# Layer 1 of a four-layer convolution kernel: weight preparation moved into the first convolution and the main loop, statistics regrouped within SBUF, one channel summed without a DMA

## The chip, the cores and the metric

The kernel runs on one core of a Trainium2 chip. The metric is the device time of the whole program in microseconds (us), from which each change is judged. One execution of the kernel before was also taken by the hardware profiler; every time below that names an engine or an instruction comes from that execution, counted from the start of its span.

## The reference, cut to what matters

Four layers follow each other on x of shape (4, 128, 64, 64), float32: an attention layer (layer 0), layer 1, a transformer-like block (layer 2) and a state-space layer (layer 3). The change touches layer 1 alone. Layer 1 is, twice, a 3x3 convolution with weights rounded to powers of two and then an "adder" convolution, each time with a batch norm behind it:

```python
def shift_quant(w, threshold=0.005):
    aw = jnp.abs(w)
    q = jnp.sign(w) * jnp.exp2(jnp.round(jnp.log2(jnp.maximum(aw, 1e-10))))
    q = jnp.where(aw < threshold, 0.0, q)
    return w + lax.stop_gradient(q - w)
...
def per_channel(wc):                       # adder_conv: p = 3x3 patches of all 128 channels
    return -jnp.sum(jnp.abs(p - wc[None, :, None]), axis=1)
...
out = adder_conv(shift_conv(x, w_shift1), w_add1)
out = jax.nn.relu(batchnorm(out, bn1_gamma, bn1_beta))     # statistics over all images and pixels
out = adder_conv(shift_conv(out, w_shift2), w_add2)
out = batchnorm(out, bn2_gamma, bn2_beta)
return jax.nn.relu(out + residual)
```

An output channel of the adder convolution sums 9 taps x 128 input channels of absolute differences for each pixel.

## The kernel before, in words

Each half of layer 1 is one call of `shift_adder`, the first with the prefix `a1`, the second with `a2`; the prefixes stand in the tile names of the profile. The three places that the change touches are where layer 0 hands over to `a1`, where `a1` hands over to `a2`, and where `a2` hands over to layer 2. They are called the first, second and third edge here.

**Before `a1`.** `layer1` calls `quantized` twice: load one set of shift weights (128 x 1152, tile `a1ws`, then `a2ws`), run nine VectorE instructions on it (`quantize`, L266 to L278), leave the result in `a1wq`, `a2wq`. Both calls use a small pool of their own over the same addresses.

**Start of `shift_adder`.** It loads the adder weights `wa` (L306), makes six negated copies `wn` (L311), fills small constant tiles (`pick`, `third`, L316 to L320), and forms `wsum`, sums of the weights over input channels, by 16 accumulations of six one-column matmuls each (L335) that VectorE copies from PSUM (L339). A float32 matmul shows as two in the profile, so these are 192 there. `w_third` (L328, L329) is one weight plane with only every fourth output channel kept. It lies in a pool of its own, closed before the pool of the convolution's input tiles (`xin`) is opened over the same addresses.

**Convolution of image 0.** `convolution(0)` is a generator: for each of 8 blocks of 512 pixels it fetches rows (`xin`, three buffers; in `a2` `normed` scales them on VectorE, L574, and ScalarE, L575), issues nine matmuls, yielding after each, and copies the block from PSUM into the padded image `pb` (L380). Image 0's runs by itself. Those of images 1 to 3 run beside the main loop.

**Main loop.** It goes over 4 images x 128 output channels, four channels at a time, in the order that the list `ORDER` writes out by hand. ScalarE makes absolute differences (`aa`, L456), VectorE makes maxima (`da`, L470; `ma`, L479; and L462), and TensorE sums each stream over the input channels with one-hot `pick` weights into PSUM (`pa`, L425). For the two `PAIR_TAPS` of a channel, `pair` makes two `ma` tiles for each half image, and a DMA issued by GpSimd adds one to the other (L481), so that TensorE need sum only one. An entry `0C0` of `ORDER` advances three steps of `beside`: the 12 steps of `sums_of_p` (a matmul sum over the image itself) and the 72 of the next image's convolution. There are 31 such entries per image that find work allowed, so 93 steps, of which 84 are used on images 0 to 2.

**Evacuation and statistics.** After 32 channels (a chunk) `evacuate` adds `wsum` and `sps` to each PSUM half (L437), takes `bn_stats` (L440) and stores to `y1d` or `y2d` in DRAM (L442). After the last chunk `batchnorm_scale` stores the statistics tile to DRAM (`stats_d`, L543), loads it back regrouped by channel (`byco`, L546), aggregates it (L550) and forms the scale `sc` (L83, L84, L553).

**Order.** A scheduler places instructions by readiness and by order in the program; `tc.keep_in_program_order` (called `then`) pins an instruction behind the one traced before it on its engine. [...] A pool opened over addresses of a closed pool waits for that pool's last users. [...]

Of the kernel before, what the change touches and what calls it, by code (L numbers as in the profile page):

```python
# [9 lines left out]
F32 = mybir.dt.float32  # L10
I32 = mybir.dt.int32
AF = mybir.ActivationFunctionType
ALU = mybir.AluOpType
# [248 lines left out]
def quantize(nc, sb, w, of, name):  # L262

    flat = [P, TAPS * P]
    aw = sb.tile(flat, F32, tag="qa", name=f"{name}_aw")
    nc.vector.tensor_scalar(aw.bitcast(I32), w.bitcast(I32), 0x7FFFFFFF, None, ALU.bitwise_and)  # L266

    pw = sb.tile(flat, F32, tag="qp", name=f"{name}_pw")
    nc.vector.tensor_scalar(pw.bitcast(I32), w.bitcast(I32), 0x7F800000, None, ALU.bitwise_and)
    up = sb.tile(flat, F32, tag="qu", name=f"{name}_up")  # L270
    nc.vector.scalar_tensor_tensor(up, pw, 1.4142135381698608, aw, ALU.mult, ALU.is_lt)
    nc.vector.scalar_tensor_tensor(pw, up, 1.0, pw, ALU.add, ALU.mult)
    nc.vector.scalar_tensor_tensor(pw, aw, 0.005, pw, ALU.is_ge, ALU.mult)
    sg = sb.tile(flat, I32, tag="qu", name=f"{name}_sg")
    nc.vector.tensor_scalar(sg, w.bitcast(I32), -0x80000000, None, ALU.bitwise_and)
    nc.vector.tensor_tensor(pw.bitcast(I32), pw.bitcast(I32), sg, ALU.bitwise_or)
    nc.vector.tensor_tensor(pw, pw, w, ALU.subtract)
    nc.vector.tensor_tensor(of, w, pw, ALU.add)  # L278


def quantized(tc, pool, w_shift, tag):

    nc = tc.nc
    wqs = pool.tile([P, TAPS, P], F32, name=f"{tag}wq")
    with tc.tile_pool(name=f"{tag}q", bufs=1) as qp:
        ws = qp.tile([P, TAPS * P], F32, name=f"{tag}ws")
        nc.sync.dma_start(ws, w_shift)
        quantize(nc, qp, ws, wqs.rearrange("p t o -> p (t o)"), tag)
    return wqs


def shift_adder(tc, cm, load, wqs, w_add, stats, y_d, tag):
# [10 lines left out]
    with ExitStack() as ctx:  # L303
        cp = ctx.enter_context(tc.tile_pool(name=f"{tag}c", bufs=1))
        wa = cp.tile([P, TAPS, P], F32, name=f"{tag}wa")
        nc.sync.dma_start(wa.rearrange("p t o -> p (t o)"), w_add)  # L306
        wn = {}
        for t, scale in [(t, 1.0) for t in ABS_TAPS[0]] + [(ABS_TAPS[c][i], 0.5) for c, i in HALF.items()]:
            if (t, scale) not in wn:
                wn[t, scale] = cp.tile([P, P], F32, name=f"{tag}wn{t}_{len(wn)}")  # L310
                nc.vector.tensor_scalar(wn[t, scale], wa[:, t, :], -scale, None, ALU.mult)  # L311

        pick = {}
        for v in (-1.0, -2.0):
            pick[v] = cp.tile([P, 63], F32, name=f"{tag}pick{int(-v)}")
            nc.vector.memset(pick[v], 0.0)  # L316
            nc.vector.memset(pick[v][:, 31:32], v)
        third = cp.tile([P, 32], F32, name=f"{tag}third")
        nc.vector.memset(third, 0.0)
        nc.vector.memset(third[:, 2:32:4], 1.0)  # L320
# [5 lines left out]
        with tc.tile_pool(name=f"{tag}w", bufs=1) as wt:  # L326
            w_third = wt.tile([P, P], F32, name=f"{tag}wthird")
            nc.vector.memset(w_third, 0.0)  # L328
            nc.vector.tensor_copy(w_third[:, 2:P:4], wa[:, MAX_TAPS[3], 2:P:4])  # L329
            pw = ps_c.tile([P, NC], F32, tag="cv", name=f"{tag}pw")  # L330
            for c in range(NC):
                for g in range(4):
                    for i, t in enumerate(sum_taps):
                        w = w_third if t == MAX_TAPS[3] else wa[:, t, :]
                        nc.tensor.matmul(  # L335
                            pw[32 * g : 32 * g + 32, c : c + 1], w[:, 32 * c : 32 * c + 32], cm.one_col,
                            start=(i == 0), stop=(i == len(sum_taps) - 1), skip_group_check=True,
                        )
            nc.vector.tensor_copy(wsum, pw)  # L339
# [64 lines left out]
        def beside(b, pb_of):  # L404

            yield from sums_of_p(b, pb_of[b], sp_of[b])
            if b < B - 1:
                pb_of[b + 1] = padded(b + 1)
                yield from convolution(b + 1, pb_of[b + 1])

        pb_of, sp_of = {0: padded(0)}, {}
        for _ in convolution(0, pb_of[0]):
            pass
# [19 lines left out]
        def evacuate(chunk):  # L433
            b, c = divmod(chunk, NC)
            for k in range(2):
                o = ep.tile([P, BK], F32, tag="ev", name=f"{tag}ev{b}_{c}_{k}")
                then(nc.vector.scalar_tensor_tensor(  # L437
                    o, pa_of[chunk][k], wsum[:, c : c + 1], sp_of[b][:, k, :], ALU.add, ALU.add
                ))
                then(nc.vector.bn_stats(stats[:, c, 2 * b + k, :], o))  # L440
                to = y_d[b, 32 * c : 32 * c + 32, :].rearrange("j (k g w) -> k g j w", k=2, g=4)
                nc.sync.dma_start(to[k], o)  # L442

# [29 lines left out]
        def pair(n, h):  # L473

            ms = []
            for t in PAIR_TAPS:
                mt = mp.tile([P, HL], F32, tag="am", name=f"m{tag}_{n}_{t}_{h}")
                v = view(n, t, h * H // 2, (h + 1) * H // 2)
                then(nc.vector.tensor_scalar(rows(mt), v, weight(n, t), None, ALU.max))  # L479
                ms.append(mt)  # L480
            then(nc.gpsimd.dma_start(ms[1], ms[0], accum_op=ALU.add))  # L481
            streams[n, "p", h] = (-2.0, ms[1], (h,))
# [52 lines left out]
def layer1(ctx, tc, cm, w_shift1, w_add1, g1, b1, w_shift2, w_add2, g2, b2, x1d, y1d, y2d, stats_d):  # L535
# [5 lines left out]
    def batchnorm_scale(stats, at, gamma, name):  # L541

        nc.sync.dma_start(at, stats.rearrange("p c s v -> p c (s v)"))  # L543
        byco = lp.tile([P, 4, 2 * B * 6], F32, name=f"byco{name}")
        for c in range(4):
            nc.sync.dma_start(  # L546
                byco[32 * c : 32 * c + 32], at[:, c, :].rearrange("(g j) s -> j g s", g=4)
            )
        mv = cm.pool.tile([P, 2], F32, name=f"mv{name}")
        nc.vector.bn_aggr(mv, byco.rearrange("p g s -> p (g s)"))  # L550
        sc = cm.pool.tile([P, 1], F32, name=f"sc{name}")
        cm.rstd(nc, sc, mv[:, 1:2])
        nc.vector.tensor_tensor(sc, sc, gamma, ALU.mult)  # L553
        return mv[:, 0:1], sc
# [5 lines left out]
    wq1, wq2 = quantized(tc, lp, w_shift1, "a1"), quantized(tc, lp, w_shift2, "a2")  # L560
# [6 lines left out]
    shift_adder(tc, cm, plain, wq1, w_add1, stats1, y1d, "a1")  # L567
    mean1, sc1 = batchnorm_scale(stats1, stats_d[0], vec["g1"], "1")
# [11 lines left out]
    shift_adder(tc, cm, normed, wq2, w_add2, stats2, y2d, "a2")  # L580
    mean2, sc2 = batchnorm_scale(stats2, stats_d[1], vec["g2"], "2")
# [997 lines left out]
def kernel(ctx: ExitStack, tc: tile.TileContext, i: dict, out: bass.AP):  # L1579
# [5 lines left out]
    stats_d = dp.tile([2, P, 4, 2 * B * 6], F32, name="stats_d")  # L1585
# [16 lines left out]
        i["w_shift2"], i["w_add2"], i["bn2_gamma"], i["bn2_beta"], x1d, y1d, y2d, stats_d,  # L1602
# [112 lines left out]
```

## Time and profile before

| What | us |
|---|---|
| Median of three runs | 21133.91 |
| The three runs | 21133.91, 21114.99, 21178.35 |
| Profiled execution, own time | 21155.93 |
| Span of that execution | 21154.1 |
| Layer 0's last VectorE instruction ends | 1980.1 |
| `a1`: first convolution matmul, first main-loop instruction | 2025.02, 2090.76 |
| `a2`: first convolution matmul, first main-loop instruction | 9438.45, 9504.25 |
| Last `a2` sum on TensorE starts | 16848.66 |
| First scaling of layer 2's input (L673) | 16878.51 |

The profile page gives TensorE as busy for 93% of the span, VectorE 90%, ScalarE 83%. Lines of the timeline read: start, busy time, engine, source line, operation, output <- inputs, shapes, count; in brackets the idle time of the engine before it and what ended that. Engine names with a q are sequencers, which wait for semaphores and issue DMAs.

### The profile page before, as it was taken

How to read it: one execution, taken by the hardware profiler on the slowest of the kernel's cores; microseconds unless marked ns; L12 is line 12 of the kernel's file. 1: busy time of each engine (PE TensorE's matmuls, PEld its weight loads, DVE VectorE, ACT ScalarE, POOL GpSimd, SP SyncE). 2: the span in 40 equal slices, each digit the busy share in tenths (PEclk: the TensorE clock that was granted, in tenths of full speed). 3: DMA queues.
4: the chain of work that ended last, by engine and by line, in shares of the span. 5: the costliest groups of instructions: out<-in, count | busy, mean ns of one | idle time of the engine just before them, and what ended most of it. 6: DMA issues, size and time to landing. Idle time of an engine off the chain costs nothing.

```text
span 21154.1 us, 323001 instructions
## 1 busy us (share of the span) xinstructions
PE 19660.1 (93%) x139180; PEld 6292.0 (30%) x139180; DVE 18970.2 (90%) x12273; ACT 17550.0 (83%) x9055; POOL 7577.3 (36%) x3844
## 2 busy tenths in 40 slices
PE   9998999999999999999999999999999877789998
PEld 4443222222222222222222222222222223223333
DVE  7876999999999999989999999999999887799998
ACT  5664999999999999989999999999999833466666
POOL 5665222222222222212222222222222100189998
PEclk9999999999999999999999999999999988699999
DMA  0000777777777777767777777777777710389997
GB/s 13 9 9 20 147 152 148 147 154 149 151 145 152 150 143 151 156 136 145 150 148 152 149 148 151 147 149 147 147 154 153 162 21 20 130 238 251 253 253 218
DMA packets 576191, 2970.17 MB, mean 140 GB/s; under 512 B 164572, under 2 KB 165476, under 8 KB 240804
## 3 DMA queue, kind: packets, MB, share of 16 engines
q0 software_dynamic: 296800, 2160.20, 51.0%
q1 hardware_dynamic: 277812, 787.19, 13.0%
q8 instruction: 1089, 17.84, 0.3%
q14 instruction: 346, 2.83, 0.0%
q10 hardware_dynamic: 144, 2.10, 0.0%
HBM read 662.03 MB, written 128.78 MB: 37 GB/s over the span
## 4 chain that ended last, share of the span: by engine, by line
PE 43%; issue 15%; DMA 14%; DVE 14%; ACT 11%; POOL 3%; SPq 1%; DVEq 0%; POOLq 0%; ACTq 0%
PE a1pa L425 15%; PE a2pa L425 13%; DMA ma<-ma 10%; ACT aa L456 9%; PE pe L164 4%; PE pav L207 4%; DVE h L1364 4%; DVE ma L479 3%; DVE da L470 2%; DMA du<-du_d 2%; DVE g L854 1%; POOL ma L481 1%; PE mg L1379 1%; DMA dl<-delta_d 1%; PE a1pc L375 1%
## 5 line engine op out<-in xcount | busy, mean ns | idle before, releaser
L481 POOL DMA_DIRECT2D ma<-ma x2048 | 3799.7, 1870 | 10892.9 <-DVE ma L479 7671.8
L456 ACT ACTIVATE aa<-a1pb,a1wn 128x4096 f32<-128x4096 f32 x1920 | 6959.4, 3711 | 485.5 <-PE a1pa L425 342.0
L456 ACT ACTIVATE aa<-a2pb,a2wn 128x4096 f32<-128x4096 f32 x1920 | 6964.9, 3712 | 358.9 <-PE a2pa L425 340.4
L425 PE MATMUL a1pa<-aa,a1pick 128*32 128x512 f32 x30720 | 3616.8, 600 | 84.4 <-ACT aa L456 81.3
L425 PE MATMUL a2pa<-aa,a2pick 128*32 128x512 f32 x30720 | 3617.2, 600 | 82.6 <-ACT aa L456 81.3
L470 DVE TENSOR_SCALAR da<-a2pb,a2wa 128x4096 f32<-128x4096 f32 x1408 | 3271.0, 2350 | 316.1 <-PE a2pa L425 316.1
L470 DVE TENSOR_SCALAR da<-a1pb,a1wa 128x4096 f32<-128x4096 f32 x1408 | 3269.6, 2350 | 306.8 <-PE a1pa L425 306.5
L425 PE MATMUL a1pa<-da,a1pick 128*32 128x512 f32 x22528 | 2696.1, 597 | 15.2 <-DVE da L470 15.2
L425 PE MATMUL a2pa<-da,a2pick 128*32 128x512 f32 x22528 | 2680.8, 594 | 18.0 <-DVE da L470 18.0
L479 DVE TENSOR_SCALAR ma<-a1pb,a1wa 128x2048 f32<-128x2048 f32 x2048 | 2529.8, 1282 | 71.1 <-DMA ma<-ma 71.1
L479 DVE TENSOR_SCALAR ma<-a2pb,a2wa 128x2048 f32<-128x2048 f32 x2048 | 2530.6, 1282 | 63.5 <-DMA ma<-ma 63.3
L1379 PE MATMUL mg<-h,ident 128*128 128x512 f32 x4096 | 1955.8, 615 | 214.6 <-ACT m L1388 174.0
L1364 DVE TENSOR_TENSOR_SCAN h<-da,h,dbu 128x1024 f32<-128x1024 f32 x768 | 1804.3, 2349 | 126.1 <-ACT da L1350 32.2
L425 PEld LDWEIGHTS a1pa<-aa,a1pick 128*32 128x32 f32 x30720 | 982.4, 111 | 2492.5 <-issue 2130.5
L425 PEld LDWEIGHTS a2pa<-aa,a2pick 128*32 128x32 f32 x30720 | 983.1, 111 | 2488.0 <-issue 2132.9
L425 PE MATMUL a2pa<-ma,a2pick 128*32 128x512 f32 x8192 | 1094.2, 607 | 266.0 <-DMA ma<-ma 265.8
L425 PE MATMUL a1pa<-ma,a1pick 128*32 128x512 f32 x8192 | 1096.2, 608 | 239.1 <-DMA ma<-ma 239.1
L201 POOL TENSOR_TENSOR ssum<-ssum,et 128x512 f32<-128x512 f32 x960 | 1230.0, 1281 | 233.0 <-ACT et L196 166.1
L425 PEld LDWEIGHTS a1pa<-da,a1pick 128*32 128x32 f32 x22528 | 716.9, 110 | 1747.2 <-issue 1612.4
L425 PEld LDWEIGHTS a2pa<-da,a2pick 128*32 128x32 f32 x22528 | 714.8, 110 | 1739.7 <-issue 1584.1
L462 DVE SCALAR_TENSOR_TENSOR aa<-a2pb,a2wa,aa 128x4096 f32<-128x4096 f32 x256 | 1147.4, 4482 | 81.8 <-ACT aa L456 81.7
L462 DVE SCALAR_TENSOR_TENSOR aa<-a1pb,a1wa,aa 128x4096 f32<-128x4096 f32 x256 | 1147.4, 4482 | 78.2 <-ACT aa L456 78.0
(295 smaller groups left out, 17707.1 us busy)
## 6 DMA issues: line engine op xcount, KB each, us to landing
ma<-ma POOLq DMA_DIRECT2D x2048, 1024.0 KB, 8.9
dl<-delta_d SPq DMA_DIRECT2D x256, 512.0 KB
dl<-delta_d SPq DMA_DIRECT2D x512, 256.0 KB
du<-du_d SPq DMA_DIRECT2D x256, 512.0 KB
du<-du_d SPq DMA_DIRECT2D x512, 256.0 KB
sz_d<-sz SPq DMA_DIRECT2D x64, 256.0 KB
xs_d<-xs SPq DMA_DIRECT2D x8, 2048.0 KB
delta_d<-dv SPq DMA_DIRECT2D x32, 512.0 KB
```

Of the source, the lines that this page charges most:

```text
L164: nc.tensor.matmul(pe, k[:, bass.ts(j, P)], unit[u, "q"], start=True, stop=True)
L201: nc.gpsimd.tensor_tensor(unit[u, "sum"], unit[u, "sum"], at, ALU.add)
L207: nc.tensor.matmul(unit[u, "av"], image[u // NB][2][:, j, :], at, start=(j == 0), stop=(j == NJ - 1))
L375: then(nc.tensor.matmul(pc, wqs[:, t, :], here[:, y : y + RB, x : x + W], start=(t == 0), stop=(t == TAPS - 1),))
L425: then(nc.tensor.matmul(pa[k][32 * g : 32 * g + 32, :], pick[v][:, 31 - jj : 63 - jj], d[:, bass.ts(4 * at + g, BK)], start=(n // 32, k) n ...
L456: then(nc.scalar.activation(rows(at), view(n, t), AF.Abs, bias=bias, scale=scale))
L462: then(nc.vector.scalar_tensor_tensor(rows(at), view(n, ADDED_TAP), weight(n, ADDED_TAP), rows(at), ALU.max, ALU.add))
L470: then(nc.vector.tensor_scalar(rows(dt), view(n, t), weight(n, t), None, ALU.max))
L479: then(nc.vector.tensor_scalar(rows(mt), v, weight(n, t), None, ALU.max))
L481: then(nc.gpsimd.dma_start(ms[1], ms[0], accum_op=ALU.add))
L1364: then(nc.vector.tensor_tensor_scan(t[:, cols][:, s], da[:, s], st[n, "dbu", h][:, cols][:, s], 0.0 if e % 4 == 0 else st["last"], ALU.mul ...
L1379: then(nc.tensor.matmul(pm, cm.ident, st[n, way, h][:, bass.ts(k, BK)], start=(way == 0), stop=(way == 1)))
```

## The change

It has four parts.

1. `quantize` becomes a generator that takes four `am` buffers (the main loop's pool for `ma` tiles, seven buffers) instead of a pool of its own, and `shift_adder` runs it. The first set is quantized ahead of `a1`'s first convolution. The second set's load is issued after that convolution's first matmul, and its VectorE instructions come in four portions at later matmuls of it. `a2` quantizes nothing.
2. The load of `wa`, the negated copies and `w_third` are likewise placed inside the convolution of image 0; the matmuls of `wsum` become eight steps of `beside` for image 0, behind `sums_of_p`. `pick` and `third` are filled by GpSimd instead of VectorE. `w_third` lives in a buffer of the evacuation pool.
3. The statistics no longer go through DRAM. When the last image's chunk is evacuated, four DMAs copy its rows of `stats` directly into `byco`; the last chunk's odd two are issued by ScalarE's queue.
4. For the very last channel `pair` issues no summing DMA; both `ma` tiles become streams that TensorE sums.

```diff
-def quantized(tc, pool, w_shift, tag):
...
-def shift_adder(tc, cm, load, wqs, w_add, stats, y_d, tag):
+def quantize(tc, pool, w_shift, of, name):
     nc = tc.nc
+    then = tc.keep_in_program_order
+    w, aw, pw, up = [
+        pool.tile([P, HL], F32, tag="am", name=f"{name}_q{k}")[:, 0 : TAPS * P] for k in range(4)
+    ]
+    nc.sync.dma_start(w, w_shift)
+    yield
...
+def shift_adder(tc, cm, load, wqs, shifts, w_add, stats, byco, y_d, tag):
...
-        nc.sync.dma_start(wa.rearrange("p t o -> p (t o)"), w_add)
         wn = {}
...
-            nc.vector.memset(pick[v], 0.0)
-            nc.vector.memset(pick[v][:, 31:32], v)
+            nc.gpsimd.memset(pick[v], 0.0)
+            nc.gpsimd.memset(pick[v][:, 31:32], v)
...
+        def sums_of_w(w_third):
             pw = ps_c.tile([P, NC], F32, tag="cv", name=f"{tag}pw")
             for c in range(NC):
                 for g in range(4):
...
+                    if g % 2:
+                        yield
+            then(nc.vector.tensor_copy(wsum, pw))
...
             yield from sums_of_p(b, pb_of[b], sp_of[b])
+            if b == 0:
+                yield from sums_of_w(w_third)
...
-        for _ in convolution(0, pb_of[0]):
-            pass
+        quantizing = [quantize(tc, mp, w, of, f"{tag}{k}") for k, (w, of) in enumerate(shifts)]
+        for q in quantizing[:1]:
+            for _ in q:
+                pass
+        for at, _ in enumerate(convolution(0, pb_of[0])):
+            if at == 0:
+                nc.sync.dma_start(wa.rearrange("p t o -> p (t o)"), w_add)
+                for q in quantizing[1:]:
+                    next(q)
+            if at % TAPS == 4 and at > 2 * TAPS:
+                for q in quantizing[1:]:
+                    next(q, None)
+            if at == 2 * TAPS + 1:
+                negated()
+                w_third = ep.tile([P, BK], F32, tag="ev", name=f"{tag}wthird")[:, 0:P]
+                then(nc.gpsimd.memset(w_third, 0.0))
+                then(nc.vector.tensor_copy(w_third[:, 2:P:4], wa[:, MAX_TAPS[3], 2:P:4]))
...
+            if b == B - 1:
+                for g in range(4):
+                    (nc.scalar if c == NC - 1 and g % 2 else nc.sync).dma_start(
+                        byco[32 * c : 32 * c + 32, g, :],
+                        stats[32 * g : 32 * g + 32, c, :, :].rearrange("p s v -> p (s v)"),
+                    )
...
-            then(nc.gpsimd.dma_start(ms[1], ms[0], accum_op=ALU.add))
+            if n < B * P - 1:
+                then(nc.gpsimd.dma_start(ms[1], ms[0], accum_op=ALU.add))
+            else:
+                streams[n, "q", h] = (-2.0, ms[0], (h,))
             streams[n, "p", h] = (-2.0, ms[1], (h,))
...
-        nc.sync.dma_start(at, stats.rearrange("p c s v -> p c (s v)"))
-        byco = lp.tile([P, 4, 2 * B * 6], F32, name=f"byco{name}")
-        for c in range(4):
-            nc.sync.dma_start(
-                byco[32 * c : 32 * c + 32], at[:, c, :].rearrange("(g j) s -> j g s", g=4)
-            )
...
-    shift_adder(tc, cm, plain, wq1, w_add1, stats1, y1d, "a1")
+    shift_adder(tc, cm, plain, wq[0], shifts, w_add1, stats1, byco[0], y1d, "a1")
...
-    shift_adder(tc, cm, normed, wq2, w_add2, stats2, y2d, "a2")
+    shift_adder(tc, cm, normed, wq[1], (), w_add2, stats2, byco[1], y2d, "a2")
```

## Prediction

> **What bounds the kernel now.** I read the page's busy shares first, then its chain, then the timeline of each engine around the three edges, then sums over stretches of the main loop. In the main loop ScalarE and TensorE are both full, so nothing large can come from there. The edges are different: they are chains in which one engine works and the rest wait.
>
> First edge, timeline of VectorE, and below it of TensorE:
>
> ```profile
> 1984.41 0.76 DVE L266 TENSOR_SCALAR a_aw<-a1ws 128x1152 int32<-128x1152 int32 x1 [4.29 <-DMA a1ws<-in_w_shift]
> ...
> 1998.59 0.76 DVE L266 TENSOR_SCALAR a_aw<-a2ws 128x1152 int32<-128x1152 int32 x1 [3.72 <-DMA a2ws<-in_w_shift]
> ...
> 2012.76 0.91 DVE L311 TENSOR_SCALAR a1wn<-a1wa 128x128 f32<-128x128 f32 x6 [3.16 <-DMA a1wa<-in_w_add]
> ...
> 2021.01 0.16 DVE L339 COPY a1wsum<-a1pw 128x4 f32<-128x4 f32 x1 [7.24 <-PE a1pw L335]
> 2035.85 0.69 DVE L380 COPY a1pb<-a1pc 128x512 f32<-128x512 f32 x1 [14.68 <-PE a1pc L375]
> ```
> ```profile
> 2025.02 50.28 PE L375 MATMUL a1pc<-a1xin,a1wq 128*128 128x512 f32 x110 [4.04 <-DMA a1xin<-x1d]
> ```
>
> Load, quantize, load, quantize, load, sum, load, convolve, one after the other. The first quantization ends at 1994.87 (L278 starts at 1993.51, 1.36 long), yet the convolution that needs only it starts at 2025.02.
>
> Second edge: TensorE, SyncE, VectorE.
>
> ```profile
> 9413.31 1.93 PE L425 MATMUL a1pa<-ma,a1pick 128*32 128x512 f32 x8 [5.49 <-DMA ma<-ma]
> ...
> 9438.45 65.03 PE L375 MATMUL a2pc<-a2xin,a2wq 128*128 128x512 f32 x144 [5.67 <-ACT a2xin L575]
> ```
> ```profile
> 9416.84 0.34 SPq L543 DMA_DIRECT2D stats_d<-stats  x1
> ...
> 9423.03 1.75 SPq L546 DMA_DIRECT2D byco<-stats_d  x4
> 9432.85 71.13 SPq L571 DMA_DIRECT2D a2xin<-y1d  x11
> ```
> ```profile
> 9426.16 1.02 DVE L550 BATCH_NORM_AGGREGATE mv<-byco 128x2 f32<-128x192 f32 x1 [0.58 <-DMA byco<-stats_d]
> 9432.82 0.16 DVE L339 COPY a2wsum<-a2pw 128x4 f32<-128x4 f32 x1 [5.64 <-PE a2pw L335]
> ```
>
> The last sum waits for a DMA, the statistics for a round trip through DRAM (6.2 us from 9416.84 to 9423.03), and `xin` for `wsum`.
>
> Third edge: SyncE, then VectorE.
>
> ```profile
> 16852.18 1.10 SPq L543 DMA_DIRECT2D stats_d<-stats  x1
> ...
> 16860.99 0.47 SPq L623 DMA_DIRECT2D dwb<-in_dw_b  x1
> 16863.85 1.76 SPq L546 DMA_DIRECT2D byco<-stats_d  x4
> ...
> 16869.77 1.76 SPq L671 DMA_DIRECT2D x<-y2d  x4
> ```
> ```profile
> 16867.13 1.02 DVE L550 BATCH_NORM_AGGREGATE mv<-byco 128x2 f32<-128x192 f32 x1 [15.00 <-DMA byco<-stats_d]
> ...
> 16878.51 2.41 DVE L673 TENSOR_SCALAR x<-x,mv,sc 128x4096 f32<-128x4096 f32 x1 [6.44 <-DMA x<-y2d]
> ```
>
> The wait list puts SyncE's stop before L623 down to `res` (5.7 us), a 2 MB load that ScalarE issues at 16850.65. Layer 2's weight loads follow, and only then `x`.
>
> [...] SyncE's 256 KB store of 16851.57 moves its packets from 16858.60 on, when `res` is nearly through. [...] The first block takes 10.83 us (2025.02 to 2035.85), later ones 7.73, and I keep that penalty.
>
> **First edge, part by part.** The `am` pool overlaps layer 0's pools, so its first load goes where `a1ws` went, 1980.56. Nine instructions end at 1994.87. The first input rows are then long there: their load, 4.0 us in the old place, runs beside quantization. So is `wa` (3.7 us). GpSimd fills the constants beside it too. Convolution starts at 1995.0 instead of 2025.02: **-30.0**. Removed are a load and a quantization (1994.87 to 2009.07, 14.2), `wa` and its sums (11.9), the wait for `xin` (4.0). Added to VectorE within the convolution are 10.5 us of quantization, 0.91 of negation, 0.19 for `w_third`. It has 7.0 us free between block copies, the largest portion is 2.9 us, and three PSUM buffers stand between it and TensorE: nothing. Without that cover it would be 11.6 us. SyncE gets two loads ahead of later `xin` rows, which are needed 7.73 us apart: nothing. If the first load is slowed by those queued behind it, 2 us; nothing excludes 1 us of gain from an earlier landing. I take 0.
>
> **Second edge.** Before the last two channel sums, TensorE ran `ma` of 510 at 9404.95. Then come four half-image streams of eight matmuls instead of two: 4 x 0.86 = 3.4 us, no DMA awaited, the last `ma` tile being done at 9405.6. They end at 9409.4, where the old end was 9415.24. Evacuation and statistics are done at 9411.0 (before: 9416.77), 5.8 earlier. The `byco` copies leave at 9411.1, two per queue 0.5 us apart, behind a 256 KB store. No SBUF-to-SBUF copy of this size is in the trace; the load of L546 took 1.8 us from its last issue to L550. I take 2.0, keep 1.5 and 6.2 as ends, and get L550 at 9413.5 and, 3.0 us on as before, `sc` at 9416.5. Beside it GpSimd, free of `a1`'s constants at 9410.3, spends about 1.7 us on memsets; `xin` goes out at 9412.0 and lands 3.9 us later (as 9432.85 to 9436.76), at 9415.9. Scaling starts at 9416.6, the convolution 1.7 later: 9418.3 instead of 9438.45, **-20.2**. Ends -16 and -21.
>
> **Third edge.** TensorE ends 5.8 us earlier by the same four streams, at 16844.8, and `res` leaves then. It took 10.3 us (16850.65 to 16860.99), so it is through at 16855.1, with the `byco` copies just behind it and L550 at about 16856.5. SyncE still stops at the DMA eight places after `res`, now the first of twelve weight loads (0.48 us each, 5.8): `x` leaves at 16860.9, against 16869.77. **-8.9**; -12 if the stop falls among later loads, -3 if the copies wait longer.
>
> **Main loop.** The sums of weights are 192 short passes in 7.9 us (41 ns each), now in the first image of each half. TensorE has little room: over 22 groups of four channels,
>
> ```profile
> 2437.10:3691.90 1254.80, 1217.71 (x10696) 360.03 (x10692) 1180.74 (x659) 1196.39 (x331) 324.52 (x183) 0.99 0.75 151
> ...
> 7960.10:9181.60 1221.50, 1156.70 (x10564) 335.18 (x10560) 1175.42 (x652) 1196.10 (x331) 274.96 (x176) 0.99 0.76 154
> 9849.00:11121.20 1272.20, 1218.20 (x10696) 357.43 (x10692) 1185.67 (x666) 1202.38 (x338) 344.76 (x182) 0.99 0.74 149
> ...
> 15400.60:16615.20 1214.60, 1151.75 (x10564) 334.40 (x10560) 1175.23 (x651) 1195.51 (x331) 278.59 (x176) 0.99 0.77 154
> ```
>
> (stretch and its length, then the busy times of PE, PEld, DVE, ACT and POOL). Image 0, with a convolution beside it, took 33 us longer than image 3 in `a1` for 61 us more of TensorE, 58 longer for 66 in `a2`: a beside-step costs 0.55 to 0.87 of its own time. Since 84 + 8 = 92 of 93 steps are used, the eight new ones fall into groups that had none. Price 7.9 x 0.55 + 7.9 x 0.87 = **+11**, between 0 and 16. The twelve early `byco` copies go out on an idle SyncE: nothing, 3 us if that cover is gone.
>
> **Sum.** -30.0 - 20.2 - 8.9 + 11 = -48. On the profiled execution's 21155.93 that is 21108. That execution lay 22 above the median 21133.91; from the median it is **21086**.
>
> **Rivals.**
> 1. *The sums are free.* TensorE has waits for DMAs of `ma` (5.49 us above) into which they may fall, and the stop at the third edge may land later. -30 - 20.2 - 12 + 0 = -62: 21072. For it: such waits recur in the loop. Against: the two stretches above.
> 2. *The DRAM trip becomes a queue.* ScalarE's two copies lie behind `res` and SyncE's behind a store: -16 and -3 at the later edges, -49 + 11 = -38: 21096. The late packets speak for it; at the second edge there is no `res`.
> 3. *Slower: the main loop falls out of step.* The `am` buffers start in another order and the convolution runs eight steps later, so the sums by DMA (median 8.9 us to land) may meet TensorE's queue at worse moments. Equal images already take 1826 to 1857 us from one group to the same one of the next image. If all six with a convolution took 1857, the loop would lose 108 us: 108 - 59 = +49, 21183. It decides from 59 us lost in all, 0.23 us for each of the 256 groups of the two halves. Against: the program order inside the loop is the same, and the same scatter can help.
> 4. *It does not do what it says*: the second quantization is scheduled ahead of the convolution, losing about 14 of the 30: 21100. The pinned order speaks against it.
>
> **How the numbers follow.** Forecast 0.55, rivals 0.22, 0.12, 0.06, 0.05. A measurement of this kernel can tell about 0.3% from no change, here 63 us; runs of one program already spread over 63 us. Around each value I allow 28 us. The forecast then passes -63 in 0.33 of its cases (0.18), rival 1 in about 0.5 (0.11), the others in about 0.2 (0.04), and a loop falling into better step by the scatter named in rival 3 adds about 0.07: 0.4 faster. Slower by over 63 needs rival 3 and more: 0.03. The range of 8 in 10 runs from 21032 to 21138, holding all the values but rival 3's.
>
> **What would show it.** Right: first convolution at 1995; no DMA named in the waits of the last eight L425; L550 within 3 us of the last L440 at the second edge; `x<-y2d` leaving near 16861 less what was gained before; L335 inside the loop. Wrong: a convolution that waits for VectorE, an `xin` landing after `sc`, or an image 0 over 20 us longer in its loop.

## Result and the profile after

The changed kernel takes 21279.67 us (median of 5 runs, 21271.42 to 21294.62); in the same comparison the kernel before takes 21130.41 (5 runs). The ratio is **1.0065, 95% interval 1.0054 to 1.0076**: slower, where 21086 was forecast and 21032 to 21138 given as the range. The profiled execution took 21289.79, its span 21288.0, against 21154.1 before: 133.9 more. The edges gave most of what was forecast; the main loop took more than three times as much back.

**First edge.** Timeline of VectorE, then of TensorE, kernel after:

```profile
1994.13 1.36 DVE L284 TENSOR_TENSOR wq<-a_q,a_q 128x1152 f32<-128x1152 f32 x1
2005.90 0.69 DVE L377 COPY a1pb<-a1pc 128x512 f32<-128x512 f32 x1 [10.42 <-PE a1pc L372]
2013.63 0.69 DVE L377 COPY a1pb<-a1pc 128x512 f32<-128x512 f32 x1 [7.03 <-PE a1pc L372]
2014.24 0.90 DVE L308 TENSOR_SCALAR a1wn<-a1wa 128x128 f32<-128x128 f32 x6
```
```profile
1995.69 64.25 PE L372 MATMUL a1pc<-a1xin,wq 128*128 128x512 f32 x144 [21.04 <-issue]
```

One quantization ahead of the convolution instead of two, no sums, one unbroken run of 144 matmuls. The main loop starts at 2060.71 instead of 2090.76, 30.05 earlier.

**Second edge.** TensorE, SyncE, VectorE:

```profile
9453.38 4.47 PE L439 MATMUL a1pa<-ma,a1pick 128*32 128x512 f32 x40
9472.69 2.90 PE L372 MATMUL a2pc<-a2xin,wq 128*128 128x512 f32 x3 [14.84 <-ACT a2xin L595]
```
```profile
9456.98 2.29 SPq L456 DMA_DIRECT2D y1d<-a1ev  x2
9459.42 1.26 SPq L460 DMA_DIRECT2D byco<-stats  x2
9460.73 2.82 SPq L591 DMA_DIRECT2D a2xin<-y1d  x2
```
```profile
9458.70 0.69 DVE L454 BATCH_NORM_STATS2 stats<-a1ev 128x6 f32<-128x512 f32 x1
9467.96 1.02 DVE L568 BATCH_NORM_AGGREGATE mv<-byco 128x2 f32<-128x192 f32 x1 [8.56 <-DMA byco<-stats]
```

The last sums wait for no DMA, and no trip to DRAM is left, but VectorE still stands 8.56 us for the copies. From the last group's L483 to the convolution it is 25.59 us instead of 39.77: 14.2 saved. (In nine of the other profiles below it is 24.7 to 24.8, and VectorE stands 7.7.)

**Third edge.** SyncE and VectorE:

```profile
16983.08 0.49 SPq L641 DMA_DIRECT2D dww<-in_dw_w  x1
16988.84 0.47 SPq L634 DMA_DIRECT2D dwb<-in_dw_b  x1
...
16996.54 2.21 SPq L691 DMA_DIRECT2D x<-y2d  x4
```
```profile
16995.38 1.02 DVE L568 BATCH_NORM_AGGREGATE mv<-byco 128x2 f32<-128x192 f32 x1 [16.43 <-DMA pww<-in_pos_w]
...
17004.54 2.41 DVE L693 TENSOR_SCALAR x<-x,mv,sc 128x4096 f32<-128x4096 f32 x1 [5.12 <-DMA x<-y2d]
```

ScalarE's queue, and a line of SyncE's wait list (who waited for whom: us in total, times, longest):

```profile
16977.47 0.38 ACTq L690 DMA_DIRECT2D res<-x1d  x1
16991.88 1.17 ACTq L460 DMA_DIRECT2D byco<-stats  x2
```
```profile
SPq L691 <- DVE mv L568: 1.4, 1, 1.4
```

SyncE still stops (16983.57 to 16988.84; the wait list names `res`, 5.2 us; at its eighth DMA counted from the one that it issues beside `res`, as in the kernel before, where it stopped 5.7 us at L623), and `x` leaves 19.07 us after `res` (16977.47), as before (16850.65 to 16869.77: 19.12). From the last L483 to L693 it is 37.9 us instead of 44.4: 6.5 saved. What holds `x` is now the statistics: the wait list puts its load behind L568, and in all twelve profiles of kernels with the change it leaves 0.13 us after L568's end (1.6 to 1.7 in the four without). L568 is late because the copies are. SyncE's two leave at 16979.65, move their packets beside the 256 KB store and `res` until 16991.17, and complete at 16991.80; ScalarE's two leave from 16991.88, 0.08 us after that, and land at 16994.75 and 16995.17. (The 16.43 us that the line puts down to `pww` end with these copies; L568 does not read `pww`.)

**Main loop.** Here the time went. First start of L491 to the last L483: 7386.4 us in `a1` instead of 7307.9, 7428.1 in `a2` instead of 7329.8, together 177 more. All of it lies in image 0 of each half. Summed over stretches of the kernel after (stretch, its length, busy times of PE, PEld, DVE, ACT and POOL, TensorE's granted clock, DMA share, GB/s), images 0 and 1 of `a1` and images 0 and 1 of `a2`:

```profile
2060.71:3981.30 1920.59, 1767.21 (x15704) 522.87 (x15708) 1704.96 (x948) 1737.74 (x480) 544.14 (x266) 0.96 0.70 142
3981.30:5807.20 1825.90, 1756.57 (x15620) 518.67 (x15616) 1717.30 (x956) 1741.70 (x482) 471.35 (x268) 0.99 0.75 151
...
9538.50:11480.10 1941.60, 1776.76 (x15704) 522.49 (x15708) 1710.45 (x956) 1744.61 (x488) 561.87 (x266) 0.96 0.70 140
11480.10:13327.20 1847.10, 1763.21 (x15624) 517.33 (x15620) 1723.35 (x963) 1748.87 (x490) 501.99 (x268) 0.99 0.74 149
```

Image 0 is 95 us longer than image 1 in both halves (before: 1825.84 and 1835.00 in `a1`), but TensorE is only 11 and 14 us busier, and VectorE and ScalarE are not busier at all: they wait. TensorE's granted clock is lower in the two slow stretches (0.96, before 0.98), but TensorE's whole busy time there is only 10 and 24 us above before (1757.66 and 1753.20), so I put no more than that down to the clock. GpSimd looks busier, by 73 and 60 us, and that too is waiting, as the next part shows.

**One slow group.** I call four channels a group, timed from its second L483 to the next group's, and number the groups of an image from 1. In `a1`'s image 0 before they take 54 to 62 us. After, eleven of 32 take 66 to 69, ten in `a2`. Here is the 13th of `a1`, kernel after: VectorE, GpSimd, TensorE.

```profile
2861.61 0.69 DVE L377 COPY a1pb<-a1pc 128x512 f32<-128x512 f32 x1 [2.63 <-PE a1pc L372]
2862.21 4.87 DVE L500 TENSOR_SCALAR ma<-a1pb,a1wa 128x2048 f32<-128x2048 f32 x4
...
2899.06 2.36 DVE L491 TENSOR_SCALAR da<-a1pb,a1wa 128x4096 f32<-128x4096 f32 x1
2912.47 2.35 DVE L491 TENSOR_SCALAR da<-a1pb,a1wa 128x4096 f32<-128x4096 f32 x1 [11.05 <-PE a1pa L439]
```
```profile
2885.84 15.70 POOL L503 DMA_DIRECT2D ma<-ma  x1 [10.68 <-DVE ma L500]
```
```profile
2907.80 1.93 PE L439 MATMUL a1pa<-ma,a1pick 128*32 128x512 f32 x8 [10.26 <-DMA ma<-ma]
```

VectorE waits 2.63 us for the last matmul of a convolution block. Its lead over TensorE is gone, so it no longer pauses for free buffers. From 2861.6 to 2901.4 it runs without a gap. GpSimd's issue of a summing DMA, at most 2.3 us long in 1912 of 2044 cases, starts at 2885.84 and ends at 2901.54, 0.12 us after VectorE stops. The sum lands late, TensorE stands 10.26 us before the stream that needs it, and VectorE then waits 11.05 for TensorE.

The same pairing is in every slow group. In the kernel after 27 groups take over 66 us; each has an issue of 15.7 to 15.9 us and a TensorE wait of 10.2 to 10.3. Before there are 7 of them, with the same two numbers; that the starved issue is what makes a group slow rests on this pairing. Of 2044 issues after, 96 take over 5 us, and all 96 end within 0.3 us after VectorE falls idle, half of them within 0.12; before 93 of 94. Where VectorE stands in its own work when an issue ends shows the same: 881 issues end while it runs L491 or L500, 878 of them within 0.15 us of the end of the instruction before; the 561 that end in an L483 do so from 0.00 to 2.17 us after its start, half of them later than 1.24. So under L491 and L500 issues end at the boundaries, under L483 inside the instruction. What in L491 and L500 keeps GpSimd waiting, no trace here shows.

**Why image 0 alone.** An entry `0C0` runs three steps. A block's copy (L377 after, L380 before) is issued by the step behind its ninth matmul. Before, `sums_of_p` took 12 steps and a block 9, so a block's last matmul was always the third of its entry, and the copy came a whole group later. The eight steps of the weight sums are no multiple of three: behind them that matmul is the second of its entry, the copy follows it at once, and VectorE has to wait for it. Images 1 and 2 have no sums of weights and keep the old place. What VectorE waited for ahead of the copies, before and then after:

```profile
  PE a1pc L375: 63.9, 8
  PE a2pc L375: 56.8, 8
```
```profile
  PE a2pc L372: 75.0, 15
  PE a1pc L372: 67.0, 15
```

(us, times). Eight of each are the convolution that runs by itself. Beside the loop no copy waited before; after, seven of eight do in image 0 of each half, 2.6 us each. The eighth falls into group 25, right behind an evacuation; it does not wait, and its group takes 61.9 and 60.4 us, not 68.

### The profile page after: what moved, and what is told of

The parts are those of the page before. It is cut to its first block, busy times and chain, and to the rows that moved or that the text cites. A ratio compares the mean times of both kernels' runs of the same rounds, so it can differ in the third digit from the quotient of the medians.

```text
span 21288.0 us, 323087 instructions
## 1 busy us (share of the span) xinstructions
PE 19684.3 (92%) x139212; PEld 6294.1 (30%) x139212; DVE 18965.3 (89%) x12259; ACT 17547.0 (82%) x9055; POOL 7682.0 (36%) x3854
## 4 chain that ended last, share of the span: by engine, by line
PE 45%; DMA 15%; DVE 14%; issue 13%; ACT 10%; POOL 3%; SPq 1%; POOLq 0%; DVEq 0%; ACTq 0%
PE a1pa L439 16%; PE a2pa L439 14%; DMA ma<-ma 11%; ACT aa L477 8%; PE pe L164 4%; PE pav L207 4%; DVE h L1384 3%; DVE ma L500 3%; DVE da L491 3%; DMA du<-du_d 2%; DVE g L874 1%; DVE aa L483 1%; PE mg L1399 1%; POOL dbu L1363 1%; POOL ma L503 1%
## 5 line engine op out<-in xcount | busy, mean ns | idle before, releaser
L503 POOL DMA_DIRECT2D ma<-ma x2044 | 3905.2, 1926 | 10912.7 <-DVE ma L500 7707.1
L491 DVE TENSOR_SCALAR da<-a2pb,a2wa 128x4096 f32<-128x4096 f32 x1408 | 3271.4, 2351 | 392.2 <-PE a2pa L439 392.1
L491 DVE TENSOR_SCALAR da<-a1pb,a1wa 128x4096 f32<-128x4096 f32 x1408 | 3269.6, 2351 | 377.5 <-PE a1pa L439 377.5
L500 DVE TENSOR_SCALAR ma<-a2pb,a2wa 128x2048 f32<-128x2048 f32 x2048 | 2531.7, 1283 | 61.4 <-DMA ma<-ma 60.9
L500 DVE TENSOR_SCALAR ma<-a1pb,a1wa 128x2048 f32<-128x2048 f32 x2048 | 2530.5, 1284 | 54.9 <-DMA ma<-ma 54.9
L483 DVE SCALAR_TENSOR_TENSOR aa<-a2pb,a2wa,aa 128x4096 f32<-128x4096 f32 x256 | 1147.6, 4483 | 87.0 <-ACT aa L477 86.8
L483 DVE SCALAR_TENSOR_TENSOR aa<-a1pb,a1wa,aa 128x4096 f32<-128x4096 f32 x256 | 1147.7, 4483 | 84.0 <-ACT aa L477 83.9
```

Source lines behind the costliest of these rows:

```text
L483: then(nc.vector.scalar_tensor_tensor(rows(at), view(n, ADDED_TAP), weight(n, ADDED_TAP), rows(at), ALU.max, ALU.add))
L491: then(nc.vector.tensor_scalar(rows(dt), view(n, t), weight(n, t), None, ALU.max))
```

## Experiments

Every ratio is against the kernel before on the same chip, with its 95% interval. **Theory 1** is the chain just told: place in the entry, wait of VectorE, starved issue. Its rivals are that the passes inside the loop cost the time by themselves, and that the later convolution does.

**A ninth, empty step behind the sums**, so that blocks again end with an entry; nothing else changes.

```diff
                 yield from sums_of_w(w_third)
+                yield
```

> The changed kernel with one empty step more behind the eight steps of the weight sums, so that the convolution of image 1 begins again with the first step of a 0C0 entry. No work is taken away. Theory 1 (where the block ends fall): with 8 steps the last matmul of a block and the PSUM copy behind it (L377) come in one entry, VectorE waits 2.6 us for it, then runs without a pause, and GpSimd cannot finish its DMA issue; a ninth step brings the block ends back to entry ends. The slow groups of image 0 from the seventh on (68 us, every third) go back to 54 to 60: 60 to 80 us less in each half, the whole 130 to 160 less than the changed kernel's 21280, some 21135. Theory 2 (the sums' own work of 7.9 us a half, and three fuller groups): no change, 21280. Theory 3 (quantizing left the am buffers in another order): no change, 21280. The first five groups of image 0 (67, 68, 60, 67, 61) lie before the sums and stay slow in all three.

Measured: 21059.5 us, ratio 1.0012 (1.0003 to 1.0021). An empty step that only delays the convolution takes back most of the loss. Image 0 falls to 1845.9 and 1870.8 us. No L377 waits in it but the last (3.49 us), which the ninth step pushes to the end of the image, and the copy of `wsum` (1.89). The 31st and 7th groups, where these two fall, are the ones behind the start that stay slow (69.7 and 68.1 in `a1`, 68.7 and 67.8 in `a2`).

**The sums ahead of the loop again**, as before the change; everything else of it stays.

```diff
-            if b == 0:
-                yield from sums_of_w(w_third)
...
+        for _ in sums_of_w(w_third):
+            pass
+
         streams, begun = {}, set()
```

> The changed kernel with the weight sums run between the convolution of image 0 and the main loop, everything else as changed. Theory 1: image 0 of both halves loses its slow groups (at least those from the seventh on), at the price of 7.9 us ahead of each loop: 21280 - 150 + 16 = 21146; if the first five groups are slow because TensorE's instruction stream ahead of the loop has changed (192 rows less), they recover too, and it is 21095. Theory 2: the loop loses 177 us against before because of the sums, so all of it comes back: 21280 - 177 + 16 = 21119. Theory 3: the loop stays as slow: 21296.

Measured: 21000.42 us, ratio 0.9976 (0.9969 to 0.9982), faster than both kernels. The rest of the change is worth 47 us, near what I had put on all of it.

**The kernel before with two empty steps ahead of each convolution in the loop**; nothing is added that an engine executes.

```diff
             if b < B - 1:
+                for _ in range(2):
+                    yield
                 pb_of[b + 1] = padded(b + 1)
```

> The kernel before with two empty steps between the sums over the image and the next image's convolution, for images 0 to 2 of both halves: no instruction is added or taken, only the convolution's matmuls move by two steps. Theory 1: every third group of three images in two halves becomes slow, 60 to 80 us for each of six images: 21130 + 360 to 480, 21490 to 21610. Theories 2 and 3: nothing, 21130.

Measured: 21378.02 us, ratio 1.0161 (1.0145 to 1.0177), 330 us more by the medians. 44 groups take over 66 us, 40 of them every third one in images 0 to 2 of both halves; image 3, without a convolution, is as before within 11 us. The waits ahead of the copies rise from 8 to 29 in each half:

```profile
  PE a1pc L375: 118.6, 29
  PE a2pc L375: 111.9, 29
```

Two empty steps thus do to three images what the sums do to one.

**The same with three empty steps**, one whole entry.

```diff
-                for _ in range(2):
+                for _ in range(3):
```

> The kernel before with three empty steps, one whole C entry of three, ahead of each convolution that runs beside a loop; no instruction is added. Theory 1 (it is the place of a block's end within its entry of three steps that decides, through the copy that VectorE waits for): three steps leave that place as it was, so the time is that of before within 20 us, the image sums stay near 1826 to 1840 us and no group of 68 us comes back every third. Theory 2 (a later convolution is what costs, whatever the place of its ends): more than the 330 us that two steps cost, images of 1880 us and over.

Measured: 21174.38 us, ratio 1.0021 (1.0013 to 1.0028). No copy in the loop waits, and seven groups take over 66 us, as before. Theory 2 falls. Still it is 44 us slower by the ratio (49 by the medians) where I allowed 20, in the profile mostly in `a2`, images 0 and 1 (1855.5 and 1857.2 us, before 1838.6 and 1839.8); what of a later convolution costs that is open.

**Three short instructions per group on VectorE**, of L483's operation, inside which 561 issues end in the kernel after; they stand in the longest stretch of L491 and L500 and are meant as pauses in which GpSimd gets in (they take the maximum of a constant tile with itself).

```diff
             streams[n, "m", i] = (-2.0, dt, (0, 1))
+            if (n % 4, i) in ((2, 2), (2, 3), (3, 1)):
+                then(nc.vector.scalar_tensor_tensor(
+                    cm.mean, cm.mean, 0.0, cm.mean, ALU.max, ALU.max
+                ))
```

> The changed kernel with three short VectorE instructions in each group of four channels (128x128 scalar_tensor_tensor on a constant that layer 1 doesn't read, values unchanged, about 0.2 us each), [...]. The block ends stay where they are. Theory 1's last link: GpSimd's issue of the ma sums is held up while VectorE runs tensor_scalar without a gap; if the short instructions let it in, issues over 5 us fall from 96 to under 20, TensorE's waits of 10.3 us go, and the slow groups with them: 21280 - 150 or more, 21130 or below, down to 20900 if the ordinary groups profit too. If they do not let it in, the 768 instructions cost up to 0.2 us each where VectorE is full: 21280 to 21430. Theories 2 and 3: 21280 to 21430.

Measured: 22087.18 us, ratio 1.0496 (1.0478 to 1.0515). A clear miss. An issue does end during the short instruction; VectorE, then GpSimd:

```profile
2894.46 0.29 DVE L494 SCALAR_TENSOR_TENSOR mean<-mean 128x128 f32<-128x128 f32 x1
```
```profile
2890.55 4.12 POOL L507 DMA_DIRECT2D ma<-ma  x1 [3.00 <-DVE ma L504]
```

The issue ends at 2894.67, within it and 0.12 us after the operation before it. But it had taken 4.12 us to get there, and elsewhere it became worse: 201 issues over 5 us instead of 96, the longest 11.2, and most groups at 59 to 63 us. So this run does not test the last link of the chain by itself. In the kernel before some 700 issues, most of about 2 us, end 0.12 us after an L470 or L479 while the next of these already runs, so an issue can end at a boundary without a gap. Which boundaries allow it, and why fewer do with these instructions added, is open.

**Sums ahead and inside, with the ninth step.**

```diff
+        for _ in sums_of_w(w_third):
+            pass
+
         streams, begun = {}, set()
...
                 yield from sums_of_w(w_third)
+                yield
```

> The changed kernel with the ninth empty step, and with the weight sums computed twice: ahead of each loop, as before, and again beside the channels. It tells what costs the first five groups of a half 24 us (67.4, 67.8, 59.6, 67.3, 60.6 us where before has 57.2, 58.8, 61.2, 58.5, 54.6). Theory 3 (the state in which the loop starts, after 192 passes fewer on TensorE, decides how the first sums fall against VectorE): with the passes ahead again the first five groups take 285 to 292 us in all. Theory 4 (the passes inside the loop cost it): they stay at 310 to 323 us. On the total: theory 3 some 15 us less a half than with the ninth step alone, less the 7 us that the passes ahead take; theory 4 some 7 us more a half than with the ninth step alone.

Measured: 21114.76 us, ratio 0.9995 (0.9986 to 1.0003). The first five groups take 294 us in `a1` and 316 in `a2`: one for each theory, so this tells nothing of them.

**Statistics ahead of the last stores.** Two kernels, both with the sums ahead of the loop. The first only moves the lines:

```diff
-                nc.sync.dma_start(to[k], o)
+                last.append((to[k], o))
+                if chunk < B * NC - 1:
+                    nc.sync.dma_start(*last.pop())
...
+            for store in last:
+                nc.sync.dma_start(*store)
```

> The changed kernel with the weight sums ahead of the loop, and in the last chunk of each half the two stores of the output issued behind the four copies of the statistics instead of ahead of them. If the copies took 8 us at the second edge because they queued behind the store: they land some 2 us after their issue, L568 starts within 4 us of the last bn_stats (8.6 before), and the first convolution of the second half 3 to 5.7 us earlier against TensorE's last sum. If the copies are slow by themselves: L568 stays over 7 us behind. At the third edge the stores become late instead, and the load of y2d, which follows them, with them: between 2 us less and 3 us more. In all 0 to 8 us under the 0.9976 of the kernel with the sums ahead.

Measured: 21060.43 us, ratio 0.9972 (0.9960 to 0.9983), no gain over the sums ahead alone. The scheduler put the stores ahead again, and VectorE waited 7.69 us for the copies, against 7.68 with the sums ahead alone. The second pins the copies, these stores and the load of `wa` with `then(...)`:

> The changed kernel with the weight sums ahead of the loop, and the two last stores of a half held behind the four copies of the statistics, this time with the order fixed on the queues (in the run before this one the program had put the stores ahead again). If the copies took 8 us because they queued behind the store: they land 2 to 4 us after their issue, L568 starts within 5 us of the last bn_stats, and the first convolution of the second half comes 3 to 6 us earlier against TensorE's last sum than with the sums ahead alone (24.7 us between the last group's start and the convolution). If it is the chunk of xin on the same queue, or the copies themselves: 0 to 2 us. At the third edge the stores of y2d are late, and the load behind them: 2 us less to 4 us more.

Measured: 21023.07 us, ratio 0.9975 (0.9965 to 0.9985); too little for the total to show, but the edges do. With the sums ahead alone, VectorE and TensorE at the second edge:

```profile
9322.71 1.02 DVE L569 BATCH_NORM_AGGREGATE mv<-byco 128x2 f32<-128x192 f32 x1 [7.68 <-DMA byco<-stats]
```
```profile
9327.44 7.93 PE L372 MATMUL a2pc<-a2xin,wq 128*128 128x512 f32 x14 [13.97 <-ACT a2xin L596]
```

and with the stores held behind the copies:

```profile
9311.29 1.02 DVE L574 BATCH_NORM_AGGREGATE mv<-byco 128x2 f32<-128x192 f32 x1 [2.85 <-DMA y1d<-a1ev]
```
```profile
9316.03 6.48 PE L372 MATMUL a2pc<-a2xin,wq 128*128 128x512 f32 x9 [9.12 <-ACT a2xin L601]
```

4.8 us less on each. From the issue at 9308.48 to L574 it is now 2.8 us; the rest was the store. At the third edge 2.1 us are gained (35.8 instead of 37.9).

**The blocks' copies on ScalarE**, in the changed kernel with its sums and steps as they are.

```diff
-                then(nc.vector.tensor_copy(pb[:, 1 + RB * k : 1 + RB * (k + 1), 1 : 1 + W], rows(pc)))
+                then(nc.scalar.copy(pb[:, 1 + RB * k : 1 + RB * (k + 1), 1 : 1 + W], rows(pc)))
```

> The changed kernel, sums and steps as it has them, with the copies of the convolution's blocks on ScalarE instead of VectorE. Theory 1 (VectorE's wait for the block's last matmul starts the cycle that ends in the starved DMA issue): the groups of 68 us every third in image 0 are gone, image 0 takes 1800 to 1850 us from its sixth group on as before, and the time falls by 100 to 150 us to about before's. Theory 5 (TensorE's order of work within the entry is what costs, and not the wait on VectorE): image 0 stays over 1900 us and the time within 40 us of the changed kernel's.

Measured: 20952.94 us, ratio 0.9911 (0.9891 to 0.9931). TensorE's order is that of the changed kernel; only VectorE no longer waits. The groups behind a copy fall from 68 to 56 us, which settles the case against TensorE's order as the cause. GpSimd and VectorE at the place shown above:

```profile
2878.14 2.08 POOL L503 DMA_DIRECT2D ma<-ma  x1 [4.83 <-DVE ma L500]
2885.87 1.84 POOL L503 DMA_DIRECT2D ma<-ma  x1 [5.64 <-DVE ma L500]
```
```profile
2880.59 2.35 DVE L491 TENSOR_SCALAR da<-a1pb,a1wa 128x4096 f32<-128x4096 f32 x1 [0.47 <-PE a1pa L439]
```

VectorE is ahead, pauses for TensorE (0.47 us from 2880.12), and the issue ends in that pause, at 2880.22. Behind the first five groups, three of which in `a1` and two in `a2` still take 67 to 68 us, only the 7th of `a1`, behind the copy of `wsum`, stays slow in image 0 (66.5). I expected about the time of before; it came out 172 us lower, since images 1 and 2, where the copies never waited, gain as well.

**The same in the kernel before**, the same line changed.

> The kernel before, with nothing of the change, and the blocks' copies on ScalarE. Theory 1: the kernel before pays for its copies as well, with groups of 59 to 61 us behind each, three images a half; they fall to 54 to 56 us, some 90 to 170 us in all, ratio 0.992 to 0.996. Theory 7 (the gain with the copies on ScalarE belongs to the change's alignment only, because there alone the copy follows at once on its matmul): within 30 us of before.

Measured: 20888.18 us, ratio 0.9904 (0.9889 to 0.9919), 201 us less. So even a copy that waits for nothing cost the kernel before: the groups behind it took 58 to 62 us, most with issues of 9 us. On ScalarE most of them take 54.8. I read it as the copy's 0.69 us using up VectorE's lead. The gain is far more than the 64 copies' own time (64 x 0.69 = 44 us), so it is not a matter of load alone.

**Both cures together.**

> Sums ahead of the loop and the blocks' copies on ScalarE, together. Theory 1 (the two losses are one mechanism, started by VectorE's waits; each cure takes away a part that the other leaves): the groups behind a copy stay at 54 to 56 us as with the copies on ScalarE alone, and the first five groups fall back to 290 us a half as with the sums ahead alone; 20 to 50 us below the copies on ScalarE alone, 0.987 to 0.990 of before. Theory 6 (the first groups depend on more than the passes ahead): the first five stay over 305 us in at least one half, and the time is within 20 us of the copies on ScalarE alone.

Measured: 20844.15 us, ratio **0.9887** (0.9872 to 0.9902), the fastest of all. In the same comparison it is 44 us under the kernel before with the copies on ScalarE: what the change gives when its sums stay outside. TensorE's waits for summing DMAs in each half, kernel after, then this one:

```profile
PE a2pa L439 <- DMA ma<-ma: 323.5, 94, 10.3
PE a1pa L439 <- DMA ma<-ma: 303.5, 74, 10.3
```
```profile
PE a2pa L440 <- DMA ma<-ma: 164.5, 67, 10.3
PE a1pa L440 <- DMA ma<-ma: 117.0, 39, 10.3
```

(us in total, times, longest).

**What costs the first five groups?** They took 323 and 322 us after, 290 and 289 before. Three kernels: one without the sums at all, the changed kernel once more, and the changed kernel with its sums computed ahead as well (no ninth step).

> The changed kernel without the weight sums (left out: the sums over the weights, whose 32 columns are set to zero): neither passes ahead of the loop nor inside it, and the convolution on the same step as before. Theory 3 (the loop's start without the 192 passes is what costs the first five groups): they take 310 to 323 us a half as in the changed kernel, the other groups of image 0 are those of before. Theory 4 (the passes inside cost it): they take 285 to 295 us. On the time: theory 3 some 20 to 45 us over the kernel with the sums ahead, theory 4 some 8 us under it.

Measured: 21029.91 us, ratio 0.9970 (0.9959 to 0.9982); first five groups 305 and 301 us, between the two theories.

> The changed kernel once more, unaltered, for a second profiled execution. If the slow first groups belong to the program: groups 1, 2 and 4 of each half take 66 to 68 us again, and so do the fifteen behind a copy. If they are chance: at least one half has its first five groups under 305 us, with the fifteen as before.

Measured: 21172.28 us, ratio 1.0049 (1.0033 to 1.0065); first five groups 294 and 297 us.

> The changed kernel with the weight sums computed ahead of each loop as well as inside it, and without the ninth empty step, so that the block ends lie where the changed kernel has them. Theory 1: the fifteen groups behind a copy stay at 66 to 69 us, whatever stands ahead of the loop. Theory 3 (the passes ahead set the start): the first five groups take 285 to 295 us in both halves, and the time is 40 to 60 us under the changed kernel's. If they are chance: over 305 us in at least one half.

Measured: 21165.48 us, ratio 1.0042 (1.0026 to 1.0059); 285 and 318 us.

The second tells most: the same program, profiled again, has the first five groups 29 and 25 us shorter, while the fifteen groups behind a wait of VectorE come back at the same places with 67.5 to 69.4 us. In the third they are there too, at 67.1 to 68.6. The fifteen belong to the program. How the first five fall changes from one execution to the next (whether on one chip is not on record), so the 66 us of the first profile are not a fixed loss of the change. That none of it belongs to the change is not shown either: over the profiles at hand, leaving out the kernel with the short instructions, they take 285 to 324 us with the sums inside the loop, ahead as well or not (twelve halves, mean 307), 284 to 305 with the sums ahead alone (eight, mean 292) and 278 to 295 without the change (eight, mean 287). What tips them is open.

## Why the prediction was wrong, step by step

- **First edge, right.** -30.0 forecast, -30.05 measured at the loop's start. VectorE's portions fitted between the block copies, and TensorE's first block was slow again, as I had assumed (10.2 us from 1995.69, the second 7.73).
- **Second edge, one term mis-sized.** -20.2 forecast, -14.2 measured. The last channel gave the 5.8 us. The copies, put at 2.0 us (my estimate, from the 1.8 us of L546's load) with ends 1.5 and 6.2, took 8.6 to L568, outside both ends. I had written that they leave behind a 256 KB store, and charged nothing for it; with the stores held behind them the same instruction comes 2.85 us after VectorE's last work.
- **Third edge, one step failed.** -8.9 forecast, -6.5 measured. The 5.8 and 0.7 in the last load are all. "`x` leaves" was to come 3 us sooner against `res`; it came at the same distance, 19.1 us. The step that failed is that the copies land just behind `res` and L550 follows 11.7 us after `res` leaves: L568 came 17.9 us after it, because ScalarE's copies left 14.4 us after `res`, and `x` waited for L568. With the stores held behind the copies ScalarE's left 8.9 us after `res`, and `x` 17.0. Rival 2 had named the two queues as the place, with -16 and -3 for the two edges; its sum, -19, was nearer than the forecast's -29.1 to the -20.7 measured.
- **Main loop, the step that failed.** +11 forecast for 192 passes, between 0 and 16; +177 measured. I priced the sums as time on TensorE, with the order inside the loop taken as unchanged. They cost as steps: eight more in a list that runs by threes. With the ends of blocks put back by an empty step, 1.0065 and 1.0049 become 1.0012. From there to the 0.9976 with the sums ahead it is 59 us by the medians. Two more slow groups in each half, behind the copy of `wsum` and the last block's copy, which also follow at once on their matmul, are 57 us longer in the one profile than in the other; what the passes themselves cost is not told apart.
- **Rival 3 had the side and half of the mechanism.** The convolution eight steps later was the cause. The order of the `am` buffers was not: `a2` quantizes nothing there and loses as much, 103 us in image 0 against 95. And the sums did not meet TensorE's queue at a worse moment: they left late, by issues of 15.7 to 15.9 us that ended only when VectorE fell idle. Its bound of 59 us lost was passed three times over, and a sign of being wrong that I had named, an image 0 over 20 us longer, showed in both halves. I gave it 0.06 on the ground that the order of the program inside the loop is the same; it was not, for the copies moved against their matmuls.
- **Balance of the two profiled executions.** Edges -50.6, loop +177, layers 2 and 3 +8: +134. Of the loop's +177, image 0 of the two halves takes +198: about 66 in the first five groups, of which 12 were left in the second execution, and 132 from the sixth on. These are the fifteen slow groups behind a wait, 207 longer than the same groups before (13.8 each), less 76 by which the other groups are shorter. The other images give 21 back.

## What to carry to other kernels

Filler work that is dealt out in fixed portions has a phase: before adding steps to it, count where each block's last producer falls in its portion and whether its consumer then follows at once on another full engine. And where GpSimd issues DMAs beside a VectorE that runs operations like L491 and L500 nearly all the time, look at VectorE's small pauses: here a copy of 0.69 us cost 4.2 us, and a wait of 2.6 us (once 1.9) went with a group 13.8 us longer. In such a kernel it is worth trying to put small copies out of PSUM on another engine (201 us less in the kernel before), and a small DMA that something waits for ahead of a large store, with the order pinned (4.8 us less at the second edge).

## What the runs showed of the hardware that I had not expected

- One GpSimd issue lasted through nine VectorE operations in a row (15.70 us, 2885.84 to 2901.54); the shortest of the same line take 0.85. Some 700 others end at the boundary of two such operations that follow each other without a gap. Both happen in one kernel.
- Moving a 0.69 us copy from VectorE to ScalarE, 64 times in the program, saved 201 us; 48 of them lie beside the loop, 4.2 us for each of these.
- With the stores held back, L574 starts 2.8 us after the first of the four 6 KB copies within SBUF that it reads is issued (9308.48 to 9311.29); behind two 256 KB stores L568 starts 8.5 us after it (9459.42 to 9467.96). The two that ScalarE's queue issued were held up as long, though the stores were not on that queue: their packets of 192 B run from 9461.48 to 9467.1, beside the stores', which end at 9467.0.
